# Columns of an adjacency matrix moved on chip instead of through DRAM, in a graph and mixture-of-experts kernel

## The chip, the core and the metric

The kernel runs on one core of one Trainium2 chip. The metric is the device time of one execution in microseconds (us); smaller is better. Three timed executions of the kernel before took 505.18, 511.95 and 511.90 us, with a median of 511.9 us. One more execution was profiled; it took 508.05 us, of which the profile's span, from the first to the last instruction, is 506.3 us. Names of engines: PE is TensorE (matrix products; its weight loads are listed apart as PEld), DVE is VectorE, ACT is ScalarE, POOL is GpSimd, SP is SyncE, which here only issues DMAs. "SPq" marks a DMA being issued by SP.

## The reference

A sparse matrix product on a graph comes first, then a mixture of experts. There are 2048 nodes with 256 features, 67,584 edges sorted by `dst`, and 8 experts with a hidden width of 1024, of which each node uses its best two.

```python
ln = _layernorm(x)                                   # 2048 x 256
gathered = edge_weight[:, None] * ln[dst]
x = x + segment_sum(gathered, src, 2048) + node_vec1 # = x + A @ layernorm(x) + bias
xt = _layernorm(x)
logits = xt @ Wr + br                                # 8 experts, the top 2 weighted by softmax
xn = layernorm(xt) * ln_g[e] + ln_b[e]
y_e = gelu(xn @ W1[e] + b1[e]) @ W2[e] + b2[e]
out = x + sum over the top 2 of weight * y_e
```

## The kernel before

**The graph part.** The kernel builds the 2048 x 2048 matrix A densely, turned so that a destination node is a column of A and sits on a partition. Columns are made in 16 blocks `cb` of 128, each in two half blocks of 64, so a loop runs over 32 half blocks `n`, with `cb = n // 2` and `h = n % 2`. One half block passes through these steps:

- `make_hots` (L299 to L327): DVE writes two one-hot tiles, `hl` (which row inside a block of 128 rows) and `eq` (which of two columns and which of 16 blocks of rows), and multiplies `eq` with the edges' weights into `hr`. The weights stand as a sum of three bf16 parts; POOL does the third part. `hl`, `eq` and `hr` have three buffers each, and step `n` of the loop makes the one-hots of half block `n + 1`.
- `make_cols` (L329 to L350): PE multiplies `hr` and `hl` in 96 small products into two PSUM tiles `pa` (three buffers, shared with other users), ACT copies each into `ar` (three buffers), and SP moves `ar` into a DRAM tile `ad` (512 KB). After the second half of a block, SP moves the whole block from `ad` back into an SBUF tile `ac` (1 MB). In `ar`, partition 32 j + 16 c + b holds column c of group j and row block b; in `ac`, the partition is the column and the rows run along it, so the two trips turn the data over.
- `dense` (L352 to L359): PE multiplies columns with layernorm(x), which lies in `xn_sb` (128 partitions, 16 blocks of 264 numbers, fp32: 256 features and 8 sums for the router). The 16 blocks `cb` form groups of 3, 3, 3, 3 and 4. An entry of the list `todo` is one group and one pair of row blocks, 6 products for a group of three; there are 8 entries for each group. `add` (L361) lets DVE add the result to `acc`.

**Order.** The loop stands under a hand-written order on all five engines: what the program states first, an engine runs first, and it never overtakes. From step `n = 8` on, each step adds 3.5 to a budget, and an entry is taken whenever its group's length fits; the last step takes what is left of the first four groups. The products of an entry are added by DVE one step later, after `make_hots(n + 2)`. After the loop there is a branch for inputs whose edges do not fit their windows (not taken here); the fifth group's entries follow behind it.

**layernorm(x).** ACT writes 4 blocks of `xn_sb` in each of the steps `n = 0` to 3 (L519), DVE its 8 router columns in step 5 (L515), from numbers that ACT copies into `acc` in step 2 (L513). `xn_sb` is first read by `dense`.

**DMAs.** All transfers named above are issued by SP, in the order of the program. A DMA waits, on the engine that issues it, for what it reads and for the completion of the transfer that last used its semaphore; there are eight such semaphores for the transfers of SP and ACT together, used in turn. Behind the loop SP issues the loads of the first experts' weights (L932 to L935), which layer 1 of the first expert (L1013) reads.

Of the kernel before, what the change touches and what calls it, by code (L numbers as in the profile page):

```python
# [9 lines left out]
F32 = mybir.dt.float32  # L10
# [11 lines left out]
P = 128  # L22
# [4 lines left out]
def kernel(  # L27
# [30 lines left out]
    nc = tc.nc  # L58
# [3 lines left out]
    NB = N // P  # L62
# [3 lines left out]
    GC = 2  # L66
# [3 lines left out]
    GB = P // GC  # L70
    GH = GB // 2
    QP = P // RK
# [8 lines left out]
    DX = D + NE  # L81
# [6 lines left out]
    dram = ctx.enter_context(tc.tile_pool(name="dram", bufs=1, space=DRAM))  # L88
# [11 lines left out]
    xn_sb = xpool.tile([P, NB, DX], F32, name="xn_sb")  # L100
# [46 lines left out]
    slot_i = consts.tile([1, NU + 2], I32, name="slot_i")  # L147
    xr_d = dram.tile([N + TS, RW], F32, name="xr_d")
    y_d = dram.tile([N + TS, D], F32, name="y_d")
    cols_d = dram.tile([NE, P, KH + 2 * KD], F32, name="cols_d")  # L150
    none = consts.tile([P, RW], F32, name="none")
    nc.vector.memset(none, 0.0)
# [25 lines left out]
    pool_of = {cb: (cols_1, cols_0)[g % 2] for g, cbs in enumerate(groups) for cb in cbs}  # L178
# [150 lines left out]
    def make_cols(n, hl, hr):  # L329


        cb, h = n // 2, n % 2
        if h == 0:
            ads[cb] = dram.tile([P, NB, P], F32, name="ad", bufs=4)
        ad_v = ads[cb].rearrange("(m j) b r -> (j b) m r", m=GB // QP)
        ar = rowsp.tile([P, GH // QP, P], F32, name="ar")
        for m0 in range(0, GH // QP, 4):
            pa = ps_a.tile([P, 4, P], F32, name="pa")
            for m in range(4):
                for i in range(3):  # L340
                    for j in range(QP):
                        g = (m0 + m) * QP + j
                        nc.tensor.matmul(pa[j * RK:(j + 1) * RK, m, :], hr[:, i, g, :],  # L343
                                         hl[:, g, :], start=(i == 0), stop=(i == 2),
                                         tile_position=(0, j * RK))
            nc.scalar.copy(ar[:, m0:m0 + 4, :], pa)  # L346
        nc.sync.dma_start(ad_v[:, h * GH // QP:(h + 1) * GH // QP, :], ar)
        if h == 1:
            acs[cb] = pool_of[cb].tile([P, NB, P], F32, name="ac")
            nc.sync.dma_start(acs[cb], ads[cb])  # L350

    def dense(cbs, b):  # L352

# [14 lines left out]
                                           acc[:, b + i, :D], op0=OP.add, op1=OP.add)  # L368
        nc.vector.tensor_add(acc[:, b:b + 2, D:], acc[:, b:b + 2, D:], pa[:, :, D:DX])

    ads, acs = {}, {}
    ET = mybir.EngineType
    ALL = {ET.DVE, ET.Pool, ET.PE, ET.Activation, ET.SP}
    with tc.manual_schedule(engines=ALL):
# [88 lines left out]
        for n in range(NH):  # L463
            q = n // 4
            f = []
            also = []
            m = n % 4
# [29 lines left out]
            make_cols(n, *hots.pop(n))  # L497


            if n >= 8:  # L500
                budget += 3.5
            while len(todo) > NB // 2 and (budget >= len(todo[0][0]) or n == NH - 1):
                cbs, b = todo.pop(0)
# [6 lines left out]
            if n < 2:  # L510
                weigh_x(2 + n)
            elif n == 2:
                nc.scalar.copy(acc[:, :, D:], xl.rearrange("p (b e) -> p b e", e=NE))  # L513
            elif n == 5:
                nc.vector.tensor_tensor(xn_sb[:, :, D:], acc[:, :, D:],  # L515
                                        rs[:, :, None].to_broadcast([P, NB, NE]), OP.mult)
            if n < 4:
                for b in range(4 * n, 4 * n + 4):
                    nc.scalar.activation(xn_sb[:, b, :D], acc[:, b, :D], AF.Identity,  # L519
                                         bias=shift[:, b:b + 1], scale=rs[:, b:b + 1])  # L520
            if n == 1:

                tr = ps_a.tile([P, 4, P], F32, name="pa").rearrange("p a b -> p (a b)")
                nt = NE * KH + 2 * NE * KD + NB
                cols = consts.tile([P, nt], F32, name="cols")
                o = 0
                for rows in (b1_rows, g_rows, be_rows, nv_rows):
                    m = rows.shape[0]
                    nc.tensor.transpose(tr[:, o:o + m], rows, ident[:m, :m])
                    o += m  # L530
                nc.scalar.copy(cols, tr[:, :nt])
                nv_c = cols[:, NE * (KH + 2 * KD):]
# [34 lines left out]
    )  # L567
    xn_d = dram.tile([N, DX], F32, name="xn_d")
    with tc.If(n_used < E):  # L569
        nc.sync.dma_start(xn_d.rearrange("(b p) d -> p b d", p=P), xn_sb)  # L570
        nc.sync.dma_start(acc[:, :, :D], xv)
        for b in range(NB):
            nc.vector.tensor_scalar(acc[:, b, :D], acc[:, b, :D], nv_c[:, b:b + 1], None,
                                    op0=OP.add)
        nc.vector.tensor_tensor(acc[:, :, D:], xn_sb[:, :, D:],
                                sd[:, :, None].to_broadcast([P, NB, NE]), OP.mult)

        for c in groups[-1]:
            nc.vector.memset(acs[c], 0.0)
        by_tile = lambda t: t.rearrange("(t p o) -> t p o", p=P, o=1)  # L580
        with tc.tile_pool(name="any", bufs=2) as anyp, tc.tile_pool(
            name="ps_any", bufs=2, space=PSUM
        ) as ps_any:
            off = anyp.tile([P, NB], F32, name="off", bufs=1)
            nc.gpsimd.iota(off, pattern=[[-P, NB]], base=0, channel_multiplier=0,
                           allow_small_or_imprecise_dtypes=True)
            with tc.For_i(0, E // P, 1) as t:
                cells = []
                for name, a, dt in (("s_t", src, I32), ("d_t", dst, I32),
                                    ("w_t", edge_weight, F32)):  # L590
                    cell = anyp.tile([P, 1], dt, name=name)
                    nc.sync.dma_start(cell, by_tile(a)[ds(t, 1)].rearrange("t p o -> (t p) o"))
                    cells.append(cell)
                s_t, d_t, w_t = cells
                g = anyp.tile([P, DX], F32, name="g")
                nc.gpsimd.indirect_dma_start(
                    out=g,
                    out_offset=None,
                    in_=xn_d[:, :],
                    in_offset=bass.IndirectOffsetOnAxis(ap=d_t, axis=0),  # L600
                )
                s_f = anyp.tile([P, 1], F32, name="s_f")
                nc.vector.tensor_copy(s_f, s_t)
                s_b = anyp.tile([P, NB], F32, name="s_b")
                nc.vector.tensor_scalar(s_b, off, s_f, None, op0=OP.add)
                for b in range(NB):
                    hot = anyp.tile([P, P], F32, name="hot")
                    nc.vector.tensor_scalar(hot, iota_p, s_b[:, b:b + 1], w_t, op0=OP.is_equal,
                                            op1=OP.mult)
                    ps = ps_any.tile([P, DX], F32, name="ps")  # L610
                    nc.tensor.matmul(ps, hot, g, start=True, stop=True)
                    nc.vector.tensor_add(acc[:, b, :], acc[:, b, :], ps)
# [600 lines left out]
```

## Time and profile before

| what | us |
|---|---|
| three timed executions | 505.18, 511.90, 511.95 |
| the profiled execution | 508.05 |
| its span | 506.3 |
| setup, before the first column transfer (`ad<-ar`) | 0 to 31.0 |
| half blocks, up to the last `ar` copy's products | to about 192 |
| remaining entries of the first four groups | 191.8 to 208.1 |
| fifth group's products | 209.5 to 239 |
| routing and experts | to 506.3 |

PE is busy in 91% of the span, DVE in 54%, ACT in 36% and POOL in 38%, but these are averages over stages: the graph part takes nearly half of the time and has different limits than the experts. The chain of waits that ended last can be followed back only to 229.95 us, so for the loop one reads the order of time and the busy time by stage instead.

In such a listing a row has the start and the length in us, the engine, the line, the operation, the tiles (output<-inputs), the shape, how many instructions were merged, and in brackets how long the engine was idle just before and what released it. Products in fp32 are listed as two records each, so "x12" on L357 is one entry of six products.

### The profile page before, as it was taken

What the parts mean: (1) busy time and instruction counts of PE and PEld (TensorE: products, weight loads), DVE (VectorE), ACT (ScalarE), POOL (GpSimd) and SP (SyncE); (2) the same over time, 40 slices, a digit from 0 to 9 for tenths busy, and PEclk for the clock granted to TensorE, in tenths of its full rate; (3) what the DMA queues carried; (4) which work ended last, traced back from release to release, by engine and by line L of the source; (5) the groups of instructions that cost most, each with busy time, mean ns of one, the idle gap of its engine ahead of it and who ended that gap; (6) DMA issues with size and microseconds to landing.
All of it is one profiled execution on the core that took longest, in us unless ns stands there. A gap on an engine that the chain in (4) does not pass through costs nothing.

```text
span 506.3 us, 12113 instructions
## 1 busy us (share of the span) xinstructions
PE 459.8 (91%) x4996; PEld 394.4 (78%) x4996; DVE 273.1 (54%) x621; ACT 183.8 (36%) x422; POOL 192.7 (38%) x158
## 2 busy tenths in 40 slices
PE   4876599898979999899999899999999999999993
PEld 3775478687758878788888788888888888888882
DVE  7999999999969971317837232323232312212111
ACT  2478524144214210028483323332243433333320
POOL 3477655544533330000142444443452444322231
PEclk9575679899979999999999999999999999999998
DMA  6128678796777667953513997997999677226420
GB/s 214 53 76 246 203 223 269 230 236 186 203 216 221 210 178 239 344 189 105 179 54 84 303 333 214 361 356 210 334 360 309 169 210 210 36 40 204 140 92 31
DMA packets 84356, 102.15 MB, mean 202 GB/s; under 512 B 8240, under 2 KB 74656, under 8 KB 82176
## 3 DMA queue, kind: packets, MB, share of 16 engines
q1 hardware_dynamic: 74832, 86.26, 53.5%
q0 software_dynamic: 7984, 13.91, 11.9%
q10 hardware_dynamic: 1472, 1.06, 0.7%
q8 instruction: 44, 0.72, 0.6%
q14 instruction: 24, 0.20, 0.1%
HBM read 75.18 MB, written 28.14 MB: 204 GB/s over the span
## 4 chain that ended last, share of the span: by engine, by line
PE 35%; DMA 13%; issue 3%; DVE 1%; SPq 0%; ACT 0%; POOL 0%; POOLq 0%; DVEq 0%
PE py L1027 16%; PE ph L1013 15%; DMA xs<-xr_d,to_i 8%; DMA y_d<-ys,to_i 2%; DMA out<-y_d 2%; PE px L978 1%; PE px L834 1%; PE py L357 1%; DMA so_far<-out,to_i 1%; DMA out<-ys,to_i 0%; SPq L1180 0%; POOL out L1048 0%; POOLq L1209 0%; ACT L1015 0%; DVE pick L957 0%
## 5 line engine op out<-in xcount | busy, mean ns | idle before, releaser
L357 PE MATMUL py<-xn_sb,ac 128*128 128x264 f32 x512 | 126.3, 404 | 1.8 <-DVEq L569 1.4
L1013 PE MATMUL ph<-xeT,w 128*128 128x256 f32 (+1 forms) x576 | 121.3, 368 | 2.4 <-PEq L1167 1.7
L1027 PE MATMUL py<-w,hT 128*128 128x256 f32 x544 | 121.0, 379 | 0.0
L1013 PEld LDWEIGHTS ph<-xeT,w 128*128 128x128 f32 x576 | 104.4, 190 | 16.5 <-issue 3.0
L357 PEld LDWEIGHTS py<-xn_sb,ac 128*128 128x128 f32 x512 | 98.5, 197 | 21.7 <-issue 2.2
L1027 PEld LDWEIGHTS py<-w,hT 128*128 128x128 f32 x544 | 101.9, 190 | 12.9
L1015 ACT ACTIVATE hT<-ph,ec 128x256 f32<-128x256 f32 (+1 forms) x144 | 66.2, 462 | 117.6 <-PE ph L1013 60.8
L1035 POOL DMA_INDIRECT y_d<-ys,to_i x30 | 48.5, 1616 | 119.3 <-DVE ys L1030 88.5
L318 POOL TENSOR_TENSOR hr<-eq,w 128x1024 bf16<-128x1024 bf16 x32 | 61.2, 1912 | 81.6 <-DVE hr L318 66.1
L343 PE MATMUL pa<-hl,hr 128*32 128x128 bf16 x3072 | 58.4, 237 | 21.6 <-POOL hr L318 10.8
L343 PEld LDWEIGHTS <-hr 128*32 128x32 bf16 x3072 | 50.0, 106 | 32.6 <-issue 14.0
L306 DVE TENSOR_TENSOR hl<-k,iota_t 128x4096 bf16<-128x4096 bf16 x32 | 72.9, 2278 | 0.0
L987 DVE TENSOR_SCALAR xeT<-px,ec 128x256 f32<-128x256 f32 (+1 forms) x38 | 18.4, 526 | 79.8 <-PE px L978 79.0
L939 POOL DMA_INDIRECT xs<-xr_d,to_i x39 | 40.5, 1038 | 54.2 <-DVE z L702 41.9
L346 ACT COPY ar<-pa 128x512 f32<-128x512 f32 x64 | 36.5, 584 | 59.8 <-PE pa L343 53.6
L1030 DVE SCALAR_TENSOR_TENSOR ys<-py,wt,b2w 128x256 f32<-128x256 f32 x34 | 16.4, 484 | 72.7 <-PE py L1027 61.3
L364 DVE TENSOR_TENSOR acc<-acc,py 128x528 f32<-128x528 f32 x32 | 22.3, 701 | 35.3 <-PE py L357 35.3
L318 DVE TENSOR_TENSOR hr<-eq,w 128x2048 bf16<-128x2048 bf16 x32 | 39.1, 1223 | 0.6
L1002 ACT ACTIVATE b2w<-b,wt 128x256 f32<-128x256 f32 x36 | 16.3, 500 | 34.0 <-DVE wt L1000 32.4
L311 DVE TENSOR_TENSOR eq<-k,iota_t 128x1024 bf16<-128x1024 bf16 x32 | 21.8, 680 | 0.0
L670 ACT ACTIVATE sq<-acc,less_m 128x256 f32<-128x256 f32 x16 | 8.0, 499 | 32.6 <-DVE acc L364 32.6
L296 ACT CAST w<-r 128x256 bf16<-128x256 f32 x16 | 6.5, 405 | 25.0 <-DVE r L295 25.0
(196 smaller groups left out, 303.0 us busy)
## 6 DMA issues: line engine op xcount, KB each, us to landing
w<-in_L_ffn_W SPq DMA_DIRECT2D x40, 1024.0 KB, 9.2
ad<-ar SPq DMA_DIRECT2D x32, 512.0 KB, 8.7
ac<-ad SPq DMA_DIRECT2D x16, 1024.0 KB, 5.9
b<-in_L_ffn_b SPq DMA_DIRECT2D x20, 128.0 KB, 9.8
out<-y_d SPq DMA_DIRECT2D x4, 512.0 KB, 6.3
xr_d<-rec SPq DMA_DIRECT2D x1, 1300.0 KB
y_d<-acc SPq DMA_DIRECT2D x1, 1280.0 KB, 5.1
acc<-in_x SPq DMA_DIRECT2D x2, 512.0 KB, 7.6
```

Source lines behind the costliest of these rows:

```text
L306: nc.vector.tensor_tensor(hl.rearrange("p g (n t) -> p g n t", t=2), two(k2[:, 0], g, P), pair(P), OP.is_equal)
L311: nc.vector.tensor_tensor(eq.rearrange("p g (n t) -> p g n t", t=2), two(k2[:, 1], g, RK), pair(RK), OP.is_equal)
L318: return engine.tensor_tensor(hr[:, i0:i1].rearrange("p i g (n t) -> p (i g) n t", t=2), eq[:, None, :, :].to_broadcast([P, i1 - i0, GH, RK]),
L343: nc.tensor.matmul(pa[j * RK:(j + 1) * RK, m, :], hr[:, i, g, :], hl[:, g, :], start=(i == 0), stop=(i == 2), tile_position=(0, j * RK))
L346: nc.scalar.copy(ar[:, m0:m0 + 4, :], pa)
L357: nc.tensor.matmul(pa[:, i, :DX], acs[c][:, b + i, :], xn_sb[:, c, :], start=(c == cbs[0]), stop=(c == cbs[-1]))
L364: nc.vector.tensor_add(acc[:, b:b + 2, :], acc[:, b:b + 2, :], pa[:, :, :DX])
L939: nc.gpsimd.indirect_dma_start(out=(sets[s.set][0] if into is None else into)[:, t, :], out_offset=None, in_=(xr_d if rows is None else ro ...
L1013: nc.tensor.matmul(ph, w1[:, k, c * P:(c + 1) * P], xeT[:, k, :], start=(k == 0), stop=(k == KD - 1))
L1015: nc.scalar.activation(hT[:, c, :s.n * P], ph, AF.Gelu, bias=ec[:, c:c + 1], scale=1.0)
L1027: nc.tensor.matmul(py, hT[:, c, t * P:(t + 1) * P], w2[:, c, :], start=(c == 0), stop=(c == KH - 1))
L1035: st = nc.gpsimd.indirect_dma_start(out=y_d[:, :], out_offset=bass.IndirectOffsetOnAxis(ap=tos[s.to][:, t:t + 1], axis=0), in_=ys, in_offs ...
```

## The change

Columns no longer pass through DRAM. After each PSUM tile is copied, four DMAs move one slice `ar[:, m, :]` each (128 partitions of 512 bytes) straight to 8 partitions of `ac`, four partitions apart (8 partitions of 16 x 512 bytes, 64 KB). A half block has eight such DMAs, six on SP's queue and two on ACT's. `ac` is allocated at the first half of a block instead of the second. The columns inside each 32 partitions thereby lie in another order, so the rows of layernorm(x) are put in the same order: `xn_sb` is written to a DRAM tile `xn_p` in four DMAs of 541 KB after step 3 and read back in permuted order in one DMA of 2.16 MB in step 5. The router columns are written in step 3 instead of 5, and entries of `todo` are taken from step 7 on instead of 8. The branch that is not taken undoes the permutation first.

```diff
+    xn_p = dram.tile([P, NB * DX], F32, name="xn_p")
+    xp = xn_p.rearrange("(q j m) f -> q m j f", m=4, j=8)
...
         if h == 0:
-            ads[cb] = dram.tile([P, NB, P], F32, name="ad", bufs=4)
-        ad_v = ads[cb].rearrange("(m j) b r -> (j b) m r", m=GB // QP)
+            acs[cb] = pool_of[cb].tile([P, NB, P], F32, name="ac")
         ar = rowsp.tile([P, GH // QP, P], F32, name="ar")
         for m0 in range(0, GH // QP, 4):
...
             nc.scalar.copy(ar[:, m0:m0 + 4, :], pa)
-        nc.sync.dma_start(ad_v[:, h * GH // QP:(h + 1) * GH // QP, :], ar)
-        if h == 1:
-            acs[cb] = pool_of[cb].tile([P, NB, P], F32, name="ac")
-            nc.sync.dma_start(acs[cb], ads[cb])
+            for m in range(m0, m0 + 4):
+                c = h * P // 2 + m0 * QP * GC + m % 4
+                queue = nc.sync if m < 6 else nc.scalar
+                queue.dma_start(acs[cb][c:c + 4 * QP * GC - 3:4], ar[:, m, :])
...
-            if n >= 8:
+            if n >= 7:
                 budget += 3.5
...
-            elif n == 5:
+            elif n == 3:
                 nc.vector.tensor_tensor(xn_sb[:, :, D:], acc[:, :, D:],
                                         rs[:, :, None].to_broadcast([P, NB, NE]), OP.mult)
+            elif n == 5:
+                nc.sync.dma_start(xn_sb.rearrange("p b d -> p (b d)"), xn_p)
             if n < 4:
                 for b in range(4 * n, 4 * n + 4):
                     nc.scalar.activation(xn_sb[:, b, :D], acc[:, b, :D], AF.Identity,
                                          bias=shift[:, b:b + 1], scale=rs[:, b:b + 1])
+            if n == 3:
+                for i in range(4):
+                    nc.sync.dma_start(xp[i], xn_sb[32 * i:32 * (i + 1)])
...
     with tc.If(n_used < E):
+        for i in range(4):
+            nc.sync.dma_start(xn_sb[32 * i:32 * (i + 1)], xp[i])
```

More of the change, by code (lines that the diff above doesn't have):

```diff
@@ L369, in add @@
         nc.vector.tensor_add(acc[:, b:b + 2, D:], acc[:, b:b + 2, D:], pa[:, :, D:DX])
-    ads, acs = {}, {}
+    acs = {}
     ET = mybir.EngineType
```

## The prediction

> **What bounds the kernel now.** I read first the busy time of each engine by stage, because the change touches only the stage of the columns. The columns of a row are the stage, its length, then busy us (instructions) of PE, PEld, DVE, ACT and POOL, PE's granted clock, the DMA share and GB/s.
>
> ```profile
> 66.00:140.00 74.00, 69.54 (x1465) 55.99 (x1457) 71.09 (x100) 25.66 (x63) 38.60 (x26) 0.96 0.78 226
> 140.00:192.00 52.00, 47.16 (x1088) 38.39 (x1087) 41.34 (x43) 13.86 (x30) 17.20 (x9) 0.93 0.71 209
> 192.00:209.00 17.00, 16.05 (x72) 13.38 (x71) 4.23 (x6) 0.47 (x1) 0.52 (x3) 1.00 0.84 274
> ```
>
> Up to 140 us DVE is the bound (71.1 of 74 us busy) with PE close behind (69.5); from 140 us on it is PE (47.2 of 52, then 16.1 of 17). The DMAs are busy in three quarters of the time but carry no engine's bound by themselves. So what can be won in 66 to 209 us is the little that is idle: 4.5 + 4.8 + 1.0 = 10.3 us of PE, and on DVE 2.9 us before 140. A stop of DVE before 140 us, on the other hand, is paid in full.
>
> Next the DMA issues, with KB for all of them and the median from issue to landing, and the list of SP's own waits:
>
> ```profile
> ad<-ar SPq DMA_DIRECT2D x32, 512.0 KB, 8.7
> ac<-ad SPq DMA_DIRECT2D x16, 1024.0 KB, 5.9
> ...
> y_d<-acc SPq DMA_DIRECT2D x1, 1280.0 KB, 5.1
> ...
> SPq L350 <- DMA ad<-ar: 102.9, 19, 9.3
> ```
>
> The trip out and back takes some 15 us, and SP's queue stands 103 us waiting for the first half of it. Who suffers from that? In the list of waits of 35 to 200 us ACT waits 5.3 us in three places for `ad<-ar`, and PE 1.2 us once for `ac<-ad`. The round trip is nearly hidden: an engine off the critical path.
>
> Last the order of time around the point where the change starts, DVE, ACT and PE:
>
> ```profile
> 47.40 2.08 ACT L519 ACTIVATE xn_sb<-acc,shift,rs 128x256 f32<-128x256 f32 x4
> ...
> 61.63 0.59 ACT L346 COPY ar<-pa 128x512 f32<-128x512 f32 x1 [2.63 <-DMA ad<-ar]
> ...
> 59.83 2.75 PE L343 MATMUL pa<-hl,hr 128*32 128x128 bf16 x96 [1.68 <-POOL hr L318]
> 63.88 2.54 PE L343 MATMUL pa<-hl,hr 128*32 128x128 bf16 x88 [1.30 <-POOL hr L318]
> 66.35 2.13 PE L357 MATMUL py<-xn_sb,ac 128*128 128x264 f32 x4
> ...
> 65.81 2.28 DVE L306 TENSOR_TENSOR hl<-k,iota_t 128x4096 bf16<-128x4096 bf16 x1
> ...
> 70.97 0.88 DVE L367 SCALAR_TENSOR_TENSOR acc<-py,cols,acc 128x256 f32<-128x256 f32 x2 [0.95 <-PE py L357]
> ```
>
> `xn_sb` is finished at 49.48 us (step 3), half block 7 leaves PE at 62.6, half block 8 at 66.35, where the first entry begins. DVE runs without a gap up to 70.0, and waits 0.95 us for that entry.
>
> **The change part by part.** The working is against the profiled execution, 508.05 us (span 506.3 and 1.75 around it); the median of the three runs is 3.85 us above it, and I carry the difference over unchanged.
>
> *What goes away.* The round trip through `ad`. Its visible price is 5.3 us of ACT's waits; ACT is busy 35% there and PE has three PSUM tiles between them, so I count 1 us. After the loop nothing is gained: at 209.45 PE waits 1.40 us for the branch (the row names L569), not for a column.
>
> *One entry sooner.* An entry is 12 records in 2.94 us at full clock. Taken in step 7 instead of after the loop it leaves the stage that PE bounds: at most 2.9 us, and I count 2.
>
> *The eight transfers of a half block.* SP issues six and ACT two; an issue of `ac<-ad` takes 0.33 us, so 2.0 us of SP and 0.7 us of ACT per half block, against (190.42 - 63.88) / 23 = 5.5 us that a half block lasts. ACT's two stand between its copies and wait for a semaphore's last transfer; behind them are the copies and the casts (L296) that DVE's `hr` needs. With ACT idle in two thirds of the stage: nothing, as long as a half block's 512 KB land within 5.5 us. The nearest row, `ad<-ar`, needs 4.4 at best and 8.7 at the median, in company of `ac<-ad`, which is gone. I take the best case, no cost; the median is the third rival. `ac` is allocated one half block earlier, so a transfer may have to wait for the old columns' last entry; entries are one step earlier too, and PE is in order: nothing.
>
> *Router columns in step 3.* DVE would write them at 43.9 us, after `hr` of half block 4, but the numbers are copied by ACT (L513) at 44.34 to 44.58: 0.7 us of DVE, covered by the next point and paid if that falls away.
>
> *layernorm(x) out and back.* This is the step that decides. It is new, 2.16 MB each way, on SP's queue between the columns, and PE's first entry needs the result. Before, nothing lay between ACT's last write and `dense` but 17 us of cover (49.48 to 66.35). Now:
>
> - Start: 49.48 plus ACT's two issues of half block 3, 0.33 each: 50.2 us.
> - Out: four DMAs of 541 KB. Low end, at the pace of `y_d<-acc` (1280 KB in 5.1 us, one such 16-block tile of 128 partitions): 2112 / 1280 x 5.1 = 8.4 us. High end, each like the median of `ad<-ar`, which has the same queue, direction, stretch and size: 4 x 8.7 = 35 us. That row is the nearest, but half of the traffic that slowed it is gone, so I stay closer to its fastest (4.4): 4 x 5.5 = 22 us, to 72.2.
> - SP then issues the way back (0.4 us), which waits for all four. The columns of half blocks 4 and 5 stand on the same queue before and beside it, those of half block 6 behind it; ACT's copy of half block 7 needs the `ar` buffer of half block 4 and waits with them.
> - Back: 2112 KB in one DMA. At the best slice of the page, 361 GB/s, it moves for 6.0 us; `ac<-ad`, which would move for 2.9 at that pace, landed in 4.9 at best, so 2.0 come on top: 8 us; at the median of `ac<-ad`, 2112 / 1024 x 5.9 = 12 us. It has 128 rows like `ac<-ad` and less company: 9 us, to 81.6.
> - PE's entry, 2.94 us at full clock or 5.59 at the halved one (the trace shows both for 12 records; after such a wait the clock may be either): 4.3 us, to 85.9.
> - DVE has made the one-hots up to half block 9 by 65.8 and then has to add this entry. It stands from 65.8 to 85.9, 20.1 us. The 0.95 us that it waited before are in it: 19 us. DVE bounds the stage, so the following work moves by that, and PE, which has half blocks 8 and 9 ready, is no further ahead than before.
>
> [...]
>
> *The weights* are now issued behind the branch (in the built order they stand after the read of the count), at 209 instead of 198.8. Three sets of 2.1 MB at the 343 GB/s of that stretch take 18.4 us and are there before 248.5, where layer 1 starts: nothing.
>
> **Sum.** 19 - 1 - 2 = +16 us: 524 against the profiled execution, 528 against the median. With four times the fastest `ad<-ar` (17.6 us out) it is 12 us, with 30 us out 24; this case alone lies in 523 to 536.
>
> **Rivals.** *Fast out and back, no change.* If the four DMAs run at the pace of `y_d<-acc`, out ends at 58.6, back at 67, the entry at 70 to 72.6: DVE waits 4.2 to 6.8 us less 0.95, the two gains take 3: 0 to 3 us more, 512 to 515. For it speaks that the DMAs are busy only to 68% in 35 to 66 us; against it `ad<-ar` itself, measured in that stretch. Chance 0.17.
>
> *Faster.* If both trips fit in the 12.4 us between 50.2 and 62.6, DVE never waits, and the 8 us of column round trip and half of the traffic are gone. At most PE's 10.3 idle us and a half of its slow clock (0.96 and 0.93 over 126 us: 6.6 us lost) are there to win, 13.6: 498 at best, and I put 500. It decides only if 2.16 MB go each way at 6.2 us, more than the best slice of the page, and SP's other transfers keep out of the way. Chance 0.07.
>
> *The columns' transfers set the pace.* If 512 KB in eight slices need more than 5.5 us, the loop runs at their pace: at 6.5 us 31 half blocks make 31 us, on top of the 16 a time of 559; at the 8.7 us of the row it would be far more. For it: 64 KB a piece, and a semaphore comes round after eight. Against: no second trip. Chance 0.08.
>
> **How the numbers follow.** The forecast, a stall of DVE at the first entry, gets the rest, 0.68. It is 528 us. The range leaves out the fast case (0.07), the paced case (0.08) and a little of the ends; it goes 4 us below the fast case, about half of what the three runs lie apart, and up to 33 us more, where out takes the 35 of the median and the rest its high ends: 508 to 545. Two per cent, 10 us, is about what a measurement of this kernel can tell from no change (its three runs lie 1.3% apart). Slower by more than that: the forecast but for a lower end (0.67) and the paced case, 0.75. Faster: 0.07. Within: 0.18.
>
> **What would show it.** Right: in the profile after, DVE waits some 20 us in one piece before L367's first add, named as waiting for PE, and PE some 19 us for a DMA `xn_sb<-xn_p`; `xn_p<-xn_sb` lands after more than 15 us; the DMA share falls from 0.78 to about half in the loop. Wrong: `xn_p<-xn_sb` lands in 8 us (first rival), or ACT's copies wait for `ac<-ar` in every half block (third), or the wait at the first entry is there but the loop ends as early as before, which would mean that DVE was not its bound.

## The result, and the profile after

| | before | after |
|---|---|---|
| timed executions: median (least to most), us | 508.86 (505.18 to 511.95, 4 runs) | 541.58 (541.06 to 543.02, 4 runs) |
| the profiled execution, us | 508.05 | 543.02 |
| its span, us | 506.3 | 541.2 |

The ratio is 1.0651, with a 95% interval of 1.0553 to 1.0748: the change makes the kernel 6.5% slower. The median of before now has one run more than the 511.9 us of the prediction. Between the two profiled executions lie 35.0 us, and those are what has to be found in the traces.

The first view is again the busy time by stage: the start and end of the stage, its length, then busy us (instructions) of PE, PEld, DVE, ACT and POOL, PE's granted clock, the DMA share and GB/s.

```profile
35.00:66.00 31.00, 21.29 (x602) 17.86 (x591) 26.18 (x34) 18.54 (x46) 17.47 (x12) 0.65 0.36 99
66.00:100.00 34.00, 2.41 (x96) 1.98 (x95) 5.90 (x6) 4.70 (x13) 6.78 (x5) 0.52 0.43 152
100.00:140.00 40.00, 34.97 (x675) 28.08 (x675) 30.98 (x51) 11.09 (x28) 14.51 (x10) 0.90 0.40 113
140.00:192.00 52.00, 50.70 (x1202) 41.30 (x1202) 51.55 (x63) 20.36 (x50) 25.04 (x16) 1.00 0.48 129
192.00:209.00 17.00, 17.00 (x344) 14.09 (x343) 16.96 (x18) 3.15 (x6) 7.51 (x4) 1.00 0.25 66
```

For comparison, the kernel before in the first of these stages:

```profile
35.00:66.00 31.00, 20.25 (x688) 17.26 (x691) 30.65 (x39) 21.32 (x54) 21.50 (x17) 0.66 0.68 202
```

Most of the loss is in the second row. From 66 to 100 us PE works for 2.4 us and DVE for 5.9 us of 34, where before they worked for 31.4 and 32.2; all engines stand. A smaller part lies ahead of it: from 35 to 66 us DVE works 4.5 us less than before. From 140 to 209 us PE and DVE are both full. This is hardly a faster loop (171.3 us from the first entry to the end of `dense`, 172.5 before): it is the work that before did some 37 us earlier, when DVE was as full (38.9 of 40 us from 100 to 140). From 100 to 192 us the DMAs are busy for 40 to 48% of the time instead of 71 to 77%. So the columns do move on chip as meant, and from 140 us on DVE and PE do not stand for them.

The second view is the list of waits between 35 and 200 us (engine, line, releaser: us in total, how often, the longest):

```profile
DVE acc L370 <- PE py L360: 36.8, 1, 36.8
ACT ar L347 <- DMA ac<-ar: 35.9, 8, 20.3
...
PE py L360 <- DMA ac<-ar: 34.6, 1, 34.6
```

DVE waits once, 36.8 us, for the first entry; PE waits once, 34.6 us, before it. The name of the DMA in PE's row is misleading. PE's first entry needs six half blocks of columns and `xn_sb`, and a wait for several semaphores is put down to one of them. What really came last is seen on SP's queue, in order of time, beside PE's first entry:

```profile
30.31 32.89 SPq L353 DMA_DIRECT2D ac<-ar  x24
63.31 5.12 SPq L529 DMA_DIRECT2D xn_p<-xn_sb  x4
68.54 24.79 SPq L353 DMA_DIRECT2D ac<-ar  x12
93.43 0.48 SPq L521 DMA_DIRECT2D xn_sb<-xn_p  x1
```

```profile
103.62 5.15 PE L360 MATMUL py<-xn_sb,ac 128*128 128x264 f32 x12 [34.63 <-DMA ac<-ar]
```

In the trace, the packets of the way out (16,896 bytes each) run from 64.9 to 87.2 us, those of the way back from 94.8 to 102.9 us, and PE starts 0.7 us after the last. Before, the first entry was at 66.35 us. It is now 37.3 us later; the last product of `dense` ends 36.0 us later (274.9 against 238.9 us), the span is 34.9 us longer. Nearly all of the loss is there at this one point, and 2.4 us of it come back, 1.3 up to the end of `dense` and 1.1 behind it.

Last, the issues of the column transfers in the answer for `ac` (least, median and greatest ns that the issuing engine spends on one):

```profile
L353 SPq DMA_DIRECT2D ac<-ar x192: 604/613/1690, 30.3 to 240.6; - x192
L353 ACTq DMA_DIRECT2D ac<-ar x64: 623/624/1234, 31.4 to 232.0; - x64
```

An issue costs 0.61 us on SP and 0.62 on ACT, where `ac<-ad` had cost 0.33: a fact of the new transfers that no row of before showed, and that matters below.

### The profile page after: what moved, and what is told of

It is laid out like the page before. It is cut to its first block, busy times and chain, and to the rows that moved or that the text cites. A ratio compares the mean times of both kernels' runs of the same rounds, so it can differ in the third digit from the quotient of the medians.

```text
span 541.2 us, 12507 instructions
## 1 busy us (share of the span) xinstructions
PE 465.3 (86%) x4996; PEld 398.4 (74%) x4996; DVE 272.5 (50%) x621; ACT 183.7 (34%) x422; POOL 192.2 (36%) x158
## 5 line engine op out<-in xcount | busy, mean ns | idle before, releaser
L360 PE MATMUL py<-xn_sb,ac 128*128 128x264 f32 x512 | 125.1, 401 | 36.7 <-DMA ac<-ar 34.6
L360 PEld LDWEIGHTS py<-xn_sb,ac 128*128 128x128 f32 x512 | 97.2, 195 | 56.8 <-issue 37.9
L1024 PEld LDWEIGHTS ph<-xeT,w 128*128 128x128 f32 x576 | 104.3, 190 | 16.6 <-issue 3.0
L1026 ACT ACTIVATE hT<-ph,ec 128x256 f32<-128x256 f32 (+1 forms) x144 | 66.2, 461 | 115.4 <-issue 62.4
L344 PE MATMUL pa<-hl,hr 128*32 128x128 bf16 x3072 | 60.8, 235 | 19.0 <-ACT ar L347 6.8
L344 PEld LDWEIGHTS <-hr 128*32 128x32 bf16 x3072 | 51.1, 104 | 31.5 <-issue 20.6
L1041 DVE SCALAR_TENSOR_TENSOR ys<-py,wt,b2w 128x256 f32<-128x256 f32 x34 | 16.4, 484 | 73.8 <-PE py L1038 63.6
L367 DVE TENSOR_TENSOR acc<-acc,py 128x528 f32<-128x528 f32 x32 | 22.2, 700 | 27.9 <-PE py L360 27.9
L370 DVE SCALAR_TENSOR_TENSOR acc<-py,cols,acc 128x256 f32<-128x256 f32 x16 | 7.0, 477 | 36.8 <-PE py L360 36.8
```

The lines of the kernel that those rows point to most:

```text
L360: nc.tensor.matmul(pa[:, i, :DX], acs[c][:, b + i, :], xn_sb[:, c, :], start=(c == cbs[0]), stop=(c == cbs[-1]))
L367: nc.vector.tensor_add(acc[:, b:b + 2, :], acc[:, b:b + 2, :], pa[:, :, :DX])
L1024: nc.tensor.matmul(ph, w1[:, k, c * P:(c + 1) * P], xeT[:, k, :], start=(k == 0), stop=(k == KD - 1))
L1026: nc.scalar.activation(hT[:, c, :s.n * P], ph, AF.Gelu, bias=ec[:, c:c + 1], scale=1.0)
```

## The experiments

The theories, as they stood: **A**, the trip of layernorm(x) to DRAM and back is the whole loss, and without it the change would be neutral or better. Its rivals: **B**, the column transfers themselves slow the loop; **C**, the placing four partitions apart is what makes the column transfers cheap, so that the permutation, and with it the trip, can't simply be dropped; and, for the part of the loss that the forecast had missed, **D**, the way out starts late, because ACT's own issues hold up ACT, and because SP, on whose queue 24 column transfers stand first, waits for semaphores that ACT's transfers hold. Since the total contains things that have nothing to do with the loop, four marks (all in us) are read from each trace: when ACT has written `xn_sb`, when PE's first entry begins, when the last product of `dense` ends, and the time from there to the end of the span. The marks come from one profiled execution of each kernel, and executions of one kernel differ by several us (before: 505.18 to 511.95), so that two marks 3 us apart are not surely different. Each ratio is against executions of before taken together with that kernel (their medians are 506.5 to 508.9).

| kernel | `xn_sb` written | first entry | `dense` ends | from there to the end | median, us | ratio to before (95%) |
|---|---|---|---|---|---|---|
| before | 49.5 | 66.4 | 238.9 | 267.4 | 508.86 | 1 |
| after | 56.2 | 103.6 | 274.9 | 266.3 | 541.58 | 1.0651 (1.0553 to 1.0748) |
| no trip | 55.0 | 67.9 | 242.4 | 293.6 | 536.03 | 1.0584 (1.0497 to 1.0671) |
| wide way out | 54.8 | 86.2 | 255.7 | 291.7 | 548.86 | 1.0864 (1.0780 to 1.0949) |
| trip in before | 50.4 | 100.3 | 268.9 | 266.6 | 536.73 | 1.0607 (1.0512 to 1.0703) |
| adjacent | 54.8 | 76.8 | 301.8 | 266.5 | 569.91 | 1.1247 (1.1139 to 1.1356) |
| columns on SP only | 51.9 | 94.3 | 271.4 | 265.8 | 538.03 | 1.0596 (1.0540 to 1.0651) |
| before, one entry sooner | 52.1 | 63.8 | 241.6 | 268.1 | 507.45 | 1.0023 (0.9993 to 1.0053) |
| wide out, GpSimd turns | 54.8 | 79.7 | 252.6 | 266.4 | 519.03 | 1.0239 (1.0205 to 1.0273) |
| late blocks only | 52.0 | 65.5 | 238.3 | 266.1 | 506.18 | 0.9981 (0.9948 to 1.0014) |
| way out on ACT | 56.2 | 99.5 | 271.5 | 265.9 | 537.66 | 1.0624 (1.0582 to 1.0667) |
| wide out on ACT, GpSimd turns | 56.1 | 77.7 | 253.5 | 266.1 | 517.93 | 1.0235 (1.0193 to 1.0277) |

**The trip taken away.** The changed kernel without the five transfers of layernorm(x). Its rows then stand in another order than the columns, so the graph sum is mixed up; that changes the routing too, and with it what the experts have to do. Only the graph part can be compared.

```diff
-            elif n == 5:
-                nc.sync.dma_start(xn_sb.rearrange("p b d -> p (b d)"), xn_p)
...
-            if n == 3:
-                for i in range(4):
-                    nc.sync.dma_start(xp[i], xn_sb[32 * i:32 * (i + 1)])
```

> The changed kernel without the five transfers of layernorm(x): it is multiplied in its old order with columns in the new one, so the graph sum is left mixed up. Theory A (the trip of layernorm(x) costs everything): the 36.8 us wait of DVE at the first entry goes, 541.6 falls by 33 to 37 to 505 to 509 us. Rival B (the 64 KB column transfers, 0.61 us of issue each and bound to each other by shared semaphores, slow the loop by themselves): at least a third of the loss stays, over 518 us.

The total, 536.0 us, lies where rival B had put it, but for a reason that neither had thought of: with another routing the experts have more to do (PE makes 672 and 592 products in their two layers instead of 576 and 544) and take 293.6 us instead of 266.3. In the graph part the answer is clear. The first entry is back at 67.9 us, and `dense` ends at 242.4 us instead of 274.9. The trip costs 32.5 of the 36.0 us; 3.5 us remain with the rest of the change. In the waits DVE's 36.8 us become 6.3:

```profile
ACT ar L347 <- DMA ac<-ar: 35.8, 11, 7.3
...
DVE acc L370 <- PE py L360: 6.3, 1, 6.3
```

ACT still waits 35.8 us for columns, now in eleven pieces, and PE is hardly held up by it. The 6.3 us are a stop of DVE at the first entry, which in step 7 comes before its last columns: PE makes a third of it at 67.9 us and goes on at 73.2. Before, DVE waited 0.95 us there, so this alone is more than the 3.5 us. That speaks for A, and against B but for 3.5 us.

**One wide transfer out.** All 128 partitions leave in one DMA; the permutation is left out, so that the graph sum is mixed up here too and only the graph part counts.

```diff
-                for i in range(4):
-                    nc.sync.dma_start(xp[i], xn_sb[32 * i:32 * (i + 1)])
+                nc.sync.dma_start(xn_p, xn_sb.rearrange("p b d -> p (b d)"))
```

> The changed kernel with the four transfers out replaced by one of 128 rows in the old order (the permutation is left out, the bytes stay); the way back is the same. Theory A1 (the narrow outermost count of 4 makes the way out long): packets of the way out end after 6 to 8 us instead of 22, and the time falls by 14 to 16 us, to 525 to 528. Rival A2 (SP's late start and the transfers ahead of the way back are most of it): less than 6 us, over 535.

The same 2.16 MB leave from 62.9 to 69.6 us: 6.7 us, where the four DMAs took 22.2 us. `dense` ends at 255.7 us, 19.2 us earlier. (The total, 548.9 us, is again that of another routing, and tells nothing for A1 or A2.) The packets are no slower in the one than in the other:

```
way out: packets of 16,896 B, landings of one DMA, mean ns of one packet, from first to last (us)
after         128    4    658    64.9 to 87.2
wide way out  128   16    670    62.9 to 69.6
```

The landings are counted in the trace: each DMA of the narrow way out adds to its semaphore four times as it lands, the wide one sixteen times. If each stands for one DMA engine at work, the packets take an estimated 128 x 0.658 / 4 = 21.1 us and 128 x 0.670 / 16 = 5.4 us, beside the 22.2 and 6.7 measured; and in after four packets of the way out are under way at once for 18.5 of its 22.2 us. The packets are as fast, then, and fewer go at once. So the shape of the way out is 19 of the trip's 32.5 us. SP's queue shows a second thing:

```profile
61.91 0.40 SPq L527 DMA_DIRECT2D xn_p<-xn_sb  x1
63.75 11.79 SPq L353 DMA_DIRECT2D ac<-ar  x12
75.59 0.65 SPq L521 DMA_DIRECT2D xn_sb<-xn_p  x1
```

The data was in DRAM at 69.6 us, and the way back was issued at 75.6: 6 us of queue.

**The trip added to before.** Columns through DRAM as before, in the natural order; layernorm(x) goes out in four DMAs whose outermost count is 4 and comes back.

```diff
+            elif n == 5:
+                nc.sync.dma_start(xn_sb.rearrange("p b d -> p (b d)"), xr[:, :8])
...
+            if n == 3:
+                for i in range(4):
+                    nc.sync.dma_start(xp[i][:, :8], xn_sb[32 * i:32 * (i + 1)])
```

> The kernel before, columns through DRAM as they were, plus the trip of layernorm(x) in the old order with the same narrow way out (four transfers, outermost count 4) after step 3 and the way back in step 5; router columns in step 3. Theory A: out starts at 50 to 52 us, takes 22, back 10, so the first entry moves from 66.3 to 83 to 86 and the time rises by 15 to 19 us over before (the sum of the prediction in its pure form). Rival B (without the small column transfers the trip is mostly hidden): under 6 us.

It was expected to cost 15 to 19 us; it cost 6.1% of 506, some 30 us. That the trip alone, without any column on chip, makes almost the whole loss is A. SP's queue and the answer for `ad` (min/median/max ns of an issue) show what made it longer than expected:

```profile
53.62 2.72 SPq L528 DMA_DIRECT2D xn_p<-xn_sb  x4
56.45 20.97 SPq L350 DMA_DIRECT2D ad<-ar  x2
83.66 0.33 SPq L353 DMA_DIRECT2D ac<-ad  x1
84.18 0.61 SPq L521 DMA_DIRECT2D xn_sb<-xn_p  x1
```

```profile
L350 SPq DMA_DIRECT2D ad<-ar x32: 359/406/20237, 31.9 to 222.5; - x32
```

The way out was issued ten us earlier than in after, but its packets began only at 58.1 us, as the `ac<-ad` ahead of them landed (58.5); they ran to 79.6, 21.5 us, as in after. The way back stood behind another `ac<-ad`, which itself waited until 83.6 for the last of the two `ad<-ar`; it was issued at 84.2 and landed at 100.2, 16 us where 10 were expected. Something new is in the second row: one issue of `ad<-ar`, the second behind the narrow transfers, kept SP for 20.24 us where the median is 0.41 (the longest in before took 5.05). It ended at 77.4, before the way out had landed, so it was not by itself what held the way back. The trace does not name what kept it.

**Eight adjacent partitions.** Each column transfer goes to 8 neighbouring partitions, in the natural order; no permutation and no trip are needed then.

```diff
-                c = h * P // 2 + m0 * QP * GC + m % 4
+                c = h * P // 2 + m * QP * GC
...
-                queue.dma_start(acs[cb][c:c + 4 * QP * GC - 3:4], ar[:, m, :])
+                queue.dma_start(acs[cb][c:c + QP * GC], ar[:, m, :])
```

> Columns on chip, but each transfer to 8 adjacent partitions in the old order, so that layernorm(x) needs no trip; entries from step 7 on. Theory A (only the trip costs): as without the trip, 505 to 509 us. Rival C (where the 8 partitions lie matters: adjacent ones land slower, so that a half block's 512 KB take longer than the 5.5 us that it lasts): the packets of 512 bytes take well over the 27 ns of the changed kernel and the loop runs at their pace, over 520 us.

569.9 us, 12.5% above before: C holds. The 512-byte packets of the columns took 61.5 ns on average on SP's queue, against 29.5 in after (27.4 for `ad<-ar` in before). The waits show what the third rival of the prediction would have looked like:

```profile
ACT ar L347 <- DMA ac<-ar: 59.8, 15, 9.9
...
DVE acc L370 <- PE py L360: 22.6, 3, 20.2
PE pa L344 <- ACT ar L347: 21.2, 6, 10.4
```

From 35 to 200 us ACT waits for columns 15 times and PE for ACT six times: here the transfers do pace the loop, which needs until 301.8 us. On average the packets were 2.1 times slower (61.5 against 29.5 ns); why, the trace does not show.

**The column transfers all on SP.** Two of eight move from ACT's queue to SP's.

```diff
-                queue = nc.sync if m < 6 else nc.scalar
+                queue = nc.sync
```

> The changed kernel with all eight column transfers on SP's queue, none on ACT's. Theory D (the late start of the way out, 13 us after the forecast, is ACT's own issues, 0.62 us each, and SP's waits for semaphores that ACT's transfers hold): DVE's 4.5 us wait in step 3 shrinks to under 1.5, the way out starts 4 us or more earlier, and the time falls by 3 to 8 us. Rival E (SP itself is too slow, eight issues of 0.66 us for a half block of 4.1 us): the way out starts no earlier and the time rises by 0 to 10 us.

ACT has `xn_sb` ready at 51.9 us instead of 56.2, and SP issues the way out at 54.9 instead of 63.3, although it has more to issue. What held SP was not the number of its transfers. In after, SP stood from 50.7 to 55.0 us and from 58.4 to 61.05 us. Both times the semaphore that its next transfer was to use had last been given to a transfer of ACT, issued at 52.8 and at 58.6 us: SP waits until ACT has come round to its issue and that transfer has landed. The way out lasts 22.2 us again (56.4 to 78.6), the first entry is 9.4 us earlier. PE's wait is named rightly in this trace:

```profile
DVE acc L370 <- PE py L360: 29.9, 1, 29.9
...
PE py L360 <- DMA xn_sb<-xn_p: 29.0, 1, 29.0
```

`dense`, however, ends only 3.5 us earlier; ACT waits 65.5 us for columns over the whole span, 55.0 in after, and that SP's queue with 256 issues is slower for the loop is my reading of it. D holds for the start. Its other signs came out in part: 538.0 us against 541.6 is a fall within its 3 to 8 us, but DVE still waits 2.3 us in step 3 (4.5 in after; under 1.5 was expected).

**Before, with entries from step 7.** One part of the change alone.

```diff
-            if n >= 8:
+            if n >= 7:
```

> The kernel before with entries taken from step 7 on, columns through DRAM. Theory: the entry is one of 2.9 us taken out of the stage that PE bounds, but its column comes back from DRAM only at some 67 us, so it gains 0 to 3 us. Rival: the early entry stops PE and through it DVE for the 4 us until the column is there, and the time rises by 1 to 4 us.

Ratio 1.0023 (0.9993 to 1.0053): the entry that is taken one step sooner brings nothing in the kernel before. Its trace (of the slowest of ten executions, 511.42 us) has the stop of which the rival spoke, for PE starts the entry at 63.8 us and then waits 5.6 us for a column on its way from DRAM:

```profile
DVE acc L367 <- PE py L357: 9.0, 1, 9.0
```

So this run shows a gain and a stop together, and not what the earlier entry is worth where the columns are there in time.

**Wide way out, and GpSimd turns it on the way back.** The permutation moves to the way back: one indirect DMA of GpSimd reads the rows in turned order, in step 6. `turn_i` holds the row number of each partition.

```diff
-            elif n == 5:
-                nc.sync.dma_start(xn_sb.rearrange("p b d -> p (b d)"), xn_p)
+            elif n == 6:
+                nc.gpsimd.indirect_dma_start(
+                    out=xn_sb.rearrange("p b d -> p (b d)"), out_offset=None, in_=xn_p,
+                    in_offset=bass.IndirectOffsetOnAxis(ap=turn_i[:, 0:1], axis=0))
...
-                for i in range(4):
-                    nc.sync.dma_start(xp[i], xn_sb[32 * i:32 * (i + 1)])
+                nc.sync.dma_start(xn_p, xn_sb.rearrange("p b d -> p (b d)"))
```

> The changed kernel with the way out as one transfer of 128 rows in the old order, and the way back as one indirect DMA of GpSimd that picks the rows in the new order in step 6; nothing is left out. Theory A1 (the narrow way out is the larger part of the loss): out takes 6 to 8 us, the graph part ends some 19 us earlier, as in the run with the wide way out, and the time is 519 to 526 us. Rival A2 (what stands ahead of the way back on its queue, not the width, sets the first entry): within 5 us of the changed kernel.

519.0 us, the lower end of what A1 expected. Out from 62.9 to 69.3 us, back from 72.3 to 79.2, the first entry at 79.7; `dense` ends 22.3 us before that of after. Waits of this kernel:

```profile
DVE acc L382 <- PE py L372: 16.2, 1, 16.2
...
PE py L372 <- DMA xn_sb<-xn_p,turn_i: 12.4, 1, 12.4
```

The columns, all on chip here, do not win back anything: the first entry is 13.3 us later than in before, and `dense` ends 13.7 us later.

**On chip only from the seventh block on.** Blocks 0 to 5 go through DRAM as before and read layernorm(x) in natural order; only blocks 6 to 15 of it are turned, out in step 6 and back in step 12, long before their first entry. The budget for entries also grows twice as much in step 8, so that entries come earlier than in before.

```diff
+            if cb >= LATE:   # LATE = 6
+                ...          # the eight transfers of the changed kernel
+                return
             ad_v = ads[cb].rearrange("(m j) b r -> (j b) m r", m=GB // QP)
...
             if n >= 8:
-                budget += 3.5
+                budget += 3.5 * (1 + (n == 8))
...
+            elif n == 6:
+                nc.sync.dma_start(xn_p, xn_sb.rearrange("p b d -> p (b d)")[:, LATE * DX:])
+            elif n == 12:
+                nc.gpsimd.indirect_dma_start(
+                    out=xn_sb.rearrange("p b d -> p (b d)")[:, LATE * DX:], out_offset=None,
+                    in_=xn_p, in_offset=bass.IndirectOffsetOnAxis(ap=turn_i[:, 0:1], axis=0))
```

> A version meant to keep the gain without the loss: the first six blocks of columns go through DRAM in the old order, blocks 6 to 15 on chip in the new one; only those blocks of layernorm(x) are turned, out in step 6 in one transfer of 128 rows, back in step 12 by an indirect DMA, well before their first entry at step 21 or so. Theory A (the loss is the trip in the way of the first entry; the columns on chip save some 8 us between half blocks 10 and 30, as the run without the trip has it): 500 to 506 us. Rival B (the column transfers cost what they save): 506 to 512.

Here no trip stands in the way, and ten of the sixteen blocks of columns stay on chip. 506.18 us over ten runs, ratio 0.9981 (0.9948 to 1.0014): no gain that could be measured, at most half a per cent. The stages of this kernel, and one of its waits from 28 to 260 us:

```profile
66.00:140.00 74.00, 65.86 (x1344) 53.45 (x1343) 65.65 (x94) 23.23 (x59) 36.67 (x25) 0.95 0.68 211
140.00:192.00 52.00, 49.63 (x1110) 40.84 (x1109) 47.09 (x52) 14.67 (x32) 19.11 (x11) 1.00 0.39 101
...
PEld py L379 <- DMA ac<-ad: 8.3, 2, 4.4
```

From 140 us on, the DMA share is 0.39 instead of 0.71, and PE was busy 2.5 us more; from 66 to 140 it was busy 3.7 us less. There PE stops twice for a block on its way from DRAM, at 66.7 and at 104.3 us, 7.5 us together (8.3 for its weight loads, in the last row), where before has 0.4. So the traffic is gone and no gain can be measured, but the kernel has two stops that before has not. How much of them the larger budget makes, and whether the kernel would be faster without it, was not tried.

**The way out on ACT's queue.** Two kernels tell the late start apart from the rest: in after, and in the version with the wide way out and the turn by GpSimd, the way out is issued by ACT, which has just written `xn_sb`. Nothing else differs.

```diff
-                    nc.sync.dma_start(xp[i], xn_sb[32 * i:32 * (i + 1)])
+                    nc.scalar.dma_start(xp[i], xn_sb[32 * i:32 * (i + 1)])
```

> The changed kernel, with the four transfers of the way out issued by ACT instead of SP; nothing else differs. Theory D (the way out starts 7 us late because SP's queue, on which column transfers wait, reaches it only 7 us after ACT wrote xn_sb at 56.23 us): ACT issues them at 56.3 to 59, they land at about 79 to 81 instead of 87.2, SP issues the way back some 4 to 6 us after that, the first entry is at 95 to 98 us instead of 103.6, the time 533 to 537 us instead of 541.6. Rival (the way out waits for the 16 engines, not for SP's queue): the packets start no earlier than 63 us, the first entry stays within 2 us of 103.6, 540 to 543 us. Second rival (ACT's own queue is blocked by the narrow transfers, so that its copies come late): ACT shows one issue of over 10 us, the first entry comes earlier, the time does not: 540 us or more.

> The version with a wide way out and a permuting way back by GpSimd (519.0 us), with the way out issued by ACT instead of SP; nothing else differs. Theory D: ACT issues it at about 55 us instead of 62.9, it lands at 62 to 63 instead of 69.3, the way back moves by as much to about 65 to 72, the first entry is at 71 to 74 us instead of 79.7, DVE waits 8 to 11 us there instead of 16.2, the time 511 to 515 us, still 1 to 1.5% above before. Rival (the way back is held by GpSimd's own place in the order, not by the way out): the first entry stays at 78 to 80, 518 to 520 us.

Both start as theory D said, and neither gives the time that it said. With the narrow way out, the packets run from 57.6 to 80.3 us, 7 us earlier, but the first entry is only 4.2 us earlier and the time 537.66 us. ACT's queue:

```profile
56.26 3.59 ACTq L529 DMA_DIRECT2D xn_p<-xn_sb  x4
...
61.71 14.38 ACTq L353 DMA_DIRECT2D ac<-ar  x2
76.13 0.40 ACT L298 CAST w<-r 128x256 bf16<-128x256 f32 x1 [14.45 <-DMA xn_p<-xn_sb]
```

The 14.38 us of the two column issues are not one long issue. Each takes 0.66 us; between them ACT stands from 62.4 to 75.4 us, because the semaphore of the second had last been given to the third transfer of the way out, which landed at 75.4. The casts and copies stand behind that, and DVE waits 15.4 us for the cast. SP in turn stands from 73.8 to 80.8 us for a column transfer that it had issued itself at 64.1: four of its eight landings were in by 66.7 us, the other four only at 80.5 to 80.8, as the last of the way out landed (80.6). Then SP has eleven column issues to make, and comes to the way back at 89.6 us. So ACT's copies do come late, as the second rival said, but not by its mark (an issue of over 10 us), and three fifths of the earlier start survived it. With the wide way out there is no such stop; the packets run from 57.0 to 62.7 us, 6 us earlier. But the turn is issued by GpSimd at 67.23 us, where its own order puts it:

```profile
65.94 0.99 POOL L247 DMA_INDIRECT win_s<-in_src,at_i  x1
67.23 1.34 POOL L533 DMA_INDIRECT xn_sb<-xn_p,turn_i  x1 [0.31 <-issue]
```

It lands from 69.4 to 77.3 us, the first entry starts 2.0 us earlier and then stops once more, 2.2 us, for columns. 517.9 against 519.0 us is no difference (ratios 1.0235 and 1.0239). The rival was right in its reason, and its numbers (78 to 80, 518 to 520) were missed by less than half a us: another queue had taken the place of SP's.

## Why the prediction was right, and where its sum was short

Direction, mechanism and place were right: one stop of DVE and PE at the first entry, made by the trip of layernorm(x), paid in full, with a loop that otherwise runs on. The measured 541.6 us lie in the range, but with some luck: its upper end was there for a way out of 35 us, and the way out took the 22 of the sum; what filled the range were waits in the queues that the sum had left out. The forecast of +16 us was half of the +35.0 us of the two profiled executions. Step by step, in the order of the sum:

| step | forecast | measured in after |
|---|---|---|
| the way out starts | 50.2 | 63.3 (issue) |
| the way out lasts | 22.0, to 72.2 | 22.2 for its packets, landed 87.2 |
| SP turns to the way back | 0.4 | 6.3, issued 93.4 |
| back | about 9, to 81.6 | 9.5, landed 102.9 |
| the first entry lasts | 4.3, to 85.9 | 5.2, to 108.8 |
| DVE stands | 20.1 | 36.8 |

The transfers themselves were sized well; the queues before them were not. That the way out met its 22.0 is luck in part too: the 5.5 us for each of its DMAs were taken from `ad<-ar`, which counts 16 landings on its semaphore, and its DMAs, with four each, landed 5.4 to 5.7 us apart. Two terms carry the error.

*"Start: 49.48 plus ACT's two issues of half block 3, 0.33 each: 50.2 us"* was 13.1 us short. ACT finished `xn_sb` at 56.2 instead of 49.5 us, and SP came to the way out 7.1 us after that. Two pairs of issues in the order of time of ACT show the first half of it:

```profile
46.31 1.45 ACTq L353 DMA_DIRECT2D ac<-ar  x2
...
49.62 0.24 ACT L516 COPY acc<-pa 128x128 f32<-128x128 f32 x1
...
52.82 1.29 ACTq L353 DMA_DIRECT2D ac<-ar  x2
54.16 2.08 ACT L524 ACTIVATE xn_sb<-acc,shift,rs 128x256 f32<-128x256 f32 x4 [1.37 <-issue]
```

Each pair of issues keeps ACT for 1.3 to 1.5 us, not 0.7, and in this stretch ACT has no slack: it sits between the casts, the copies and the last four blocks of `xn_sb`. The forecast had costed ACT's issues at nothing because ACT is idle in two thirds of the stage from 66 to 140 us; in the steps before the first entry it is not (21.3 of 31 us busy from 35 to 66 in before). Not all of the 6.7 us is the change's: the five profiled kernels in which ACT issues no column in these steps have `xn_sb` written at 49.5 to 52.1 us, before being the earliest, the seven in which it does at 54.8 to 56.2. The copy for the router columns (L516) came at 49.6 us, DVE waited for it 4.54 us and not 0.7, and that was on DVE's path. With ACT's two issues moved to SP, ACT is done at 51.9 us and the way out is issued 8.4 us earlier; with the way out on ACT's own queue it is issued as soon as `xn_sb` is written. Both show that the start was a matter of queues. Both give back part of the gain elsewhere, so the 13 us cannot simply be subtracted from the time.

*"SP then issues the way back (0.4 us)"* was 5.9 us short. The text named the columns of half blocks 4 and 5 on the same queue "before and beside it" and gave them no price. SP stood from 72.4 to 82.4 and from 83.0 to 87.9 us for the semaphores of two column transfers that ACT had issued at 67.0 and 67.6 us, behind the way out; the last came free 0.8 us after the last packet of the way out. What ties them to the way out is the time: each of the two counts eight landings on its semaphore, of which four were in by 70.7 us and the other four only at 82.0 to 82.4 and 87.7 to 87.9, just after the third and fourth transfer of the way out (81.9 and 87.5). Eight column issues followed, 0.66 us from one to the next, 5.3 us, and then the way back. In the wide version the same queue costs 6.0 us (69.6 to 75.6), and moving the way back to GpSimd brought `dense` 3.1 us forward (255.7 to 252.6), no more than two executions can differ by.

The remaining differences are small: 1.9 us between issue and landing of the way out, 1.2 from the way back's issue to the first entry, 0.9 for the entry. Together with 13.1 and 5.9 they make up the 22.9 us from 85.9 to 108.8. DVE itself came to its wait 6.2 us later than forecast (72.0 instead of 65.8), so its wait is 16.7 longer.

*"ACT's waits, 1 us"* and *"one entry sooner, 2 us"*: between the first entry and the end 2.4 us came back, which is close to 3. But 1.1 of them lie behind `dense`, where the other kernels with the same routing differ by as much, and neither source was confirmed by itself. The earlier entry alone gives nothing in before, and the stop of DVE that it brought there (9.0 us) and in the kernel without the trip (6.3) is a cost that the term had left out. The late-blocks kernel gains at most half a per cent.

*The weights behind the branch*: nothing, as said; from the end of `dense` the two kernels need 267.4 and 266.3 us.

*The eight transfers of a half block: nothing*: right for the loop from 140 us on (the third rival is false; PE and DVE are full there), wrong for the steps before the first entry, as told above. In the graph part without the trip 3.5 us remain, and there the change as a whole is no gain.

*The rivals.* The fast way out was refuted by 22.2 us for 2.16 MB. Even the wide way out did not give "no change": with 6.4 us out and 6.9 us back, late starts included, the time is 519.0 us, 2.4% above before. The faster rival named as its condition that both trips fit in before 62.6 us; the late-blocks kernel takes the trip off the path altogether, and is not faster, though with two stops of its own. What the columns' traffic could give back was small: ACT's 5.3 us of waits were nearly its only visible price.

The number of landings went with the shape of the transfer: a DMA with outermost counts 4 and 32 counted four on its semaphore, one with 128 rows sixteen, a column slice (8 and 128) eight. No other shapes were compared, so what sets the number is not shown.

The loss, then, by parts of the graph part (36.0 us): 19.2 the narrow way out; 3.1 the way back on SP's queue instead of GpSimd's; 10.2 a wide trip, with the queue ahead of it, that stands before the first entry at all (252.6 against 242.4); 3.5 the rest. The parts of 3 us are about what two executions of one kernel can differ by. The first and the second are differences between runs with mixed-up and right sums, whose graph parts do the same work. What remains open is the share of the late start, ACT's and SP's, in the 10.2 and 3.5, since every edit that moved it also changed a queue.

No version beat the kernel before; the best, late blocks only, equals it.

## What to carry to other kernels

Before a transfer is put on a path that the bound engine reads, find its place on its queue: what stands ahead, what those issues cost in *that* stage, and which shared semaphores they wait for; the queues here were 13.1 and 5.9 us of what the forecast missed, and the narrow shape of the transfer 19.2 of the loss. Then look at its shape: the same 2.16 MB left in 22.2 us by four DMAs with outermost counts 4 and 32, and in 6.7 us by one with 128 rows. And traffic that the bound engine does not wait for is not surely worth a trip of its own: with the DMA share down from 0.71 to 0.39 no gain could be measured here.

## What was not expected of the hardware

- An issue of a column DMA to 8 partitions kept SP for 0.61 us and ACT for 0.62 (medians), one of `ac<-ad` 0.33, one of `ad<-ar` 0.43 and the wide way out 0.40; the way back, with 128 rows too, 0.46 to 0.68.
- Behind four narrow transfers an issue on the same queue itself stopped in two kernels: one took 20.24 us on SP with the trip added to before (median 0.41), one 9.35 us with all columns on SP (median 0.61). In after no issue did (1.69 at most).
- 512-byte packets took 29.5 ns to partitions four apart and 61.5 ns to adjacent ones (means on SP's queue).
- From 140 to 192 us PE's granted clock was 0.93 in before and 1.00 in after. It does not follow the DMA traffic: it was 1.00 also in the two other kernels whose columns all go through DRAM (DMA share 0.76 and 0.72) and 0.93 with adjacent partitions (0.59). Why it differs is open.
- A wait that two engines share by a semaphore used in turn is invisible in the code: SP stood 14.9 us in after (72.4 to 82.4, 83.0 to 87.9) for two transfers of ACT, and ACT 13.0 us with the way out on its queue (62.4 to 75.4) for a transfer of the way out. Neither engine needed the result.
